# A graph network kernel: when three engines read its end-of-program flag, and which engine issues the last outputs

## The chip, the cores and the metric

The kernel runs on one core of a Trainium2 chip. The metric is the device time of one execution in microseconds. Three runs of the kernel before took 475.0, 475.29 and 475.76 us; their median is 475.29.

A core has five engines with an instruction queue each: TensorE (PE; its weight loads are shown as PEld), VectorE (DVE), ScalarE (ACT), GpSimd (POOL) and SyncE (SP, which only issues transfers and waits). They meet through semaphores. A "q" behind a name (SPq) marks an instruction of the engine's sequencer: a DMA issue, a wait, a branch, a register load.

## The reference

There are 2500 nodes of 256 features and 80000 edges. A layer norm and a relu are followed by three layers of an edge convolution that averages over incoming edges, and a product with the concatenation of all layers is added to the input:

```
def _edge_conv(x, src, dst, W, b):
    m = concatenate([x[dst], x[src] - x[dst]], axis=-1) @ W + b
    s = segment_sum(m, dst, num_segments=N)
    cnt = segment_sum(ones, dst, num_segments=N)
    return s / maximum(cnt, 1.0)[:, None]

h = maximum(_layernorm(x), 0.0)
xs = [h]
for W, b in ((W0, b0), (W1, b1), (W2, b2)):
    h = relu(_edge_conv(h, src, dst, W, b))
    xs.append(h)
return x + concatenate(xs, axis=-1) @ Wf + bf
```

## The kernel before

The 2500 nodes make 20 tiles of 128 rows (the last has 68), which go through the kernel as ten pairs. `by_windows` builds the matrix of edge counts from one-hot products of short stretches of the sorted edge list, keeps it in DRAM for the later layers, and runs the three layers as matrix products with it. That path holds only where no stretch has more edges than it was given room for. At about 182 us `shares` writes a single integer, the tile `missing`: 0 if all edges were found, 1 if not. At the end of the program (line 1441) `values_load` loads it into a register of each of the five engines, and `tc.If` (line 1442) branches on it: if it is 1, the engines run `general`, a slow path that holds for any graph; if it is 0, as here, they jump over that path to the closing waits. Line 1438 marks that jump as likely for TensorE, VectorE and ScalarE.

The order of work on each engine is written out by hand. `PEo`, `DVEo`, `POOLo`, `ACTo` and `SPo` are wrappers whose calls stay in program order on their engine; all of these calls are shown at line 282, the wrapper's. Calls through `nc` or the plain engines, the flag loads among them, are placed by the framework where their inputs allow: SyncE and GpSimd load the flag at 183 us already, in the midst of the program, and ScalarE, VectorE and TensorE behind their last computations. Transfers signal their landing on eight semaphores that are used in turn; before an issue the queue waits until the previous transfer on that semaphore has landed.

The change is in the last loop of `by_windows` (lines 1410 to 1431) and in `gnn_kernel`. The loop goes over the ten pairs in the order 8, 9, 0, 1, 2, 3, 7, 6, 5, 4 of `orders[L]`. For pair `q` TensorE multiplies its two tiles of the last layer's result with the last part of `Wf`, each tile into half a bank (the last pair into two banks); VectorE (`add_to_acc`) adds each product, scaled, into the tile's place in `acc`; and SyncE issues the transfer of that tile to `out`, 128 KB:

```
for k in range(2):
    t = 2 * q + k
    add_to_acc(t, po[k])
    n = P if t < NT - 1 else LAST
    SPo.dma_start(out[t * P:t * P + n, :], acc[:n, t, :])
```

During the first four pairs ScalarE and VectorE still prepare the operands of later ones. ScalarE has nothing to do after that.

Of the kernel before, what the change touches and what calls it, by code (L numbers as in the profile page):

```python
# [313 lines left out]
def by_windows(ctx: ExitStack, tc: tile.TileContext, x, src, dst, Ws, bs, Wf, bf, out, missing):  # L314
    nc = tc.nc
    PE, DVE, ACT, POOL, SP = nc.tensor, nc.vector, nc.scalar, nc.gpsimd, nc.sync
    PEo, DVEo, POOLo, ACTo, SPo = (InOrder(tc, e) for e in (PE, DVE, POOL, ACT, SP))
    P = 128
# [29 lines left out]
    Q = NT // 2  # L348
# [23 lines left out]
    def bank():  # L372
        return ps[-1].tile([P, 512], F32, name="bank")


    acc = const.tile([P, NT, D], F32, name="acc")
# [136 lines left out]
    behind = pp.tile([P, WG * P], F32, name="behind")  # L513
# [510 lines left out]
    def split_in_blocks(q, whole=True):  # L1024
        two = [block().rearrange("p c n -> p (c n)") for _ in range(2)]
        return Split(q, [two[0][:, :2 * D], two[0][:, 2 * D:], two[1][:, :2 * D]], whole)
# [93 lines left out]
    def times(to, split, i, forms):  # L1120
        for c in range(DC):
            for k in range(3):
                PEo.matmul(to, split.parts[k][:, c, i * P:(i + 1) * P], forms.parts[k][:, c, :],
                           start=(c == 0 and k == 0), stop=(c == DC - 1 and k == 2))

    def add_to_acc(t, po):
        DVEo.scalar_tensor_tensor(acc[:, t, :], po, share[:, t:t + 1], acc[:, t, :], op0=OP.mult, op1=OP.add)
# [211 lines left out]
    def split(q):  # L1339
        tile_ = stage.tile([P, 4 * GS], F32R, name="staged")  # L1340
        Split(q, [tile_[:, k * 2 * D:(k + 1) * 2 * D] for k in range(3)])

    begun = []
    for l in range(1, L):
# [7 lines left out]
        for i in range(Q + LAG):  # L1352
            if 0 < i <= Q:
                lone.make(i - 1)
            if i < Q:
                q = order[i]
                n = Nodes(l, q)
# [53 lines left out]
    for i, q in enumerate(order):  # L1411
        po = bank()
        po = [po[:, :D], bank()[:, :D] if i == Q - 1 else po[:, D:]]
        for k in range(2):
            if q in PLAIN:
                for c in range(DC):
                    PEo.matmul(po[k], hT[:, c, (2 * q + k) * P:(2 * q + k + 1) * P], wfs[L][:, c, :],
                               start=(c == 0), stop=(c == DC - 1))
            else:
                times(po[k], splits[q], k, coming[0])  # L1420
        for k in range(2):
            t = 2 * q + k
            add_to_acc(t, po[k])
            n = P if t < NT - 1 else LAST
            SPo.dma_start(out[t * P:t * P + n, :], acc[:n, t, :])
        if i == 0:
            begun[0].rest()
        elif i == 1:
            split_in_blocks(3)
        elif i < 4:  # L1430
            split((5, 4)[i - 2])


def gnn_kernel(tc: tile.TileContext, x, src, dst, Ws, bs, Wf, bf, out):
    nc = tc.nc
    with tc.tile_pool(name="flag", bufs=1) as flag:
        missing = flag.tile([1, 1], I32, name="missing")
        tc.mark_branch_hint_location("again", "LikelyTaken",
                                     engines=[getattr(mybir.EngineType, e) for e in ("PE", "DVE", "Activation")])
        by_windows(tc, x, src, dst, Ws, bs, Wf, bf, out, missing)  # L1440
        again = nc.values_load(missing, min_val=0, max_val=1)
        with tc.If(again > 0, label="again"):
            general(tc, x, src, dst, Ws, bs, Wf, bf, out)

# [27 lines left out]
```

## Time and profile before

| | |
|---|---|
| median of three runs | 475.29 us |
| the profiled execution's own time | 475.97 us |
| its span, from its first to its last instruction | 474.0 us |
| TensorE clock granted | 0.998 |
| PE busy | 462.7 us, 98% |
| DVE busy | 380.5 us, 80% |
| ACT busy | 310.6 us, 66% |
| output issues on SyncE | 20, at 454.5 to 470.2 us, 287 / 386 / 2093 ns (least, median, most) |
| from issue to landing of an output | 1.8 / 1.9 / 2.0 us |

Times inside the execution count from the span's first instruction. The 1.97 us between the profiled execution's time and its span lie outside the instructions shown. "Busy" leaves out what a sequencer does alone. A DMA issue's duration is the time its queue is held, not the transfer's; the transfer runs behind it on 16 shared DMA engines, and its landing is told by its semaphore. The view of DMA queues lists packets by queue, those that bring the engines' own instructions among them, and their share of the time of all 16 DMA engines in the stretch looked at.

### The profile page before, as it was taken

The page shows a single profiled execution, that of the slowest core. Times are in us where ns is not written, and L with a number is a line of the kernel's source. Part 1 is how long each engine was busy: PE and PEld are TensorE (multiplying, and loading weights), DVE is VectorE, ACT ScalarE, POOL GpSimd, SP SyncE. Part 2 cuts the span into 40 slices and gives each one's busy share as a digit, 9 for nine tenths or more (in the row PEclk, how much of TensorE's full clock was granted, in tenths as well). Part 3 has the DMA queues.
Part 4 walks back from the last instruction along what each step waited for, and adds up shares of the span by engine and source line. Part 5 has one row for each costly group of instructions (what it writes and reads, how often), then busy time and mean ns, then how long its engine had stood idle before and what let it go on. Part 6 is the DMA issues. An engine that isn't in the chain of part 4 may idle for free.

```text
span 474.0 us, 7362 instructions
## 1 busy us (share of the span) xinstructions
PE 462.7 (98%) x2739; PEld 365.3 (77%) x2739; DVE 380.5 (80%) x699; ACT 310.6 (66%) x543; POOL 42.6 (9%) x66
## 2 busy tenths in 40 slices
PE   7999999999999999999999999999999999999994
PEld 3787888788778878877887877877788787688694
DVE  7988988799898873499987847876999687569794
ACT  4877677686664541378769857775777797497430
POOL 2674014300101001000000000000000000000000
PEclk9999999999999999999999999999999999999999
DMA  8320073991733707532178552010213955220024
GB/s 277 90 56 1 1 157 66 187 215 35 158 63 69 152 0 152 124 100 75 46 235 310 176 174 62 28 44 5 83 44 97 360 177 176 87 88 0 1 73 147
DMA packets 21775, 52.07 MB, mean 110 GB/s; under 512 B 1943, under 2 KB 12134, under 8 KB 21734
## 3 DMA queue, kind: packets, MB, share of 16 engines
q1 hardware_dynamic: 14950, 33.93, 21.9%
q0 software_dynamic: 5856, 16.51, 18.2%
q10 hardware_dynamic: 928, 1.11, 0.7%
q8 instruction: 22, 0.36, 0.3%
q14 instruction: 19, 0.16, 0.1%
HBM read 36.08 MB, written 15.46 MB: 109 GB/s over the span
## 4 chain that ended last, share of the span: by engine, by line
PE 88%; DVE 5%; POOL 3%; DMA 2%; issue 1%; ACTq 0%; DVEq 0%; POOLq 0%
PE bank L282 84%; PE pz L282 3%; DMA acc<-in_x_dram 2%; DVE acc L282 2%; POOL acc L282 1%; DVE st L282 1%; POOL es L282 1%; POOL ed L282 1%; DVE staged L282 1%; DVE tmp L282 0%; DVE zl L282 0%; DVE mv L282 0%; PE turned L282 0%; DVE kn L282 0%; DVE rs L282 0%
## 5 line engine op out<-in xcount | busy, mean ns | idle before, releaser
L282 ACT CAST block<-staged 128x1008 fp32r<-128x1008 bf16 x120 | 117.8, 1031 | 17.0 <-DVE staged L282 6.3
L282 PE MATMUL bank<-block,zh 128*128 128x504 f32 (+1 forms) x200 | 83.7, 419 | 0.0
L282 PE MATMUL bank<-a,zh 128*128 128x504 f32 (+1 forms) x200 | 81.7, 409 | 0.0
L282 ACT CAST a<-bank 128x480 fp32r<-128x480 f32 (+1 forms) x105 | 54.5, 561 | 39.0 <-PE bank L282 37.2
L282 PE MATMUL bank<-a,zl 128*128 128x504 f32 (+1 forms) x200 | 77.8, 389 | 0.0
L282 PE MATMUL bank<-block,zl 128*128 128x504 f32 (+1 forms) x200 | 77.3, 387 | 0.0
L282 DVE TENSOR_TENSOR one_m<-iota_m,key_m 128x2048 bf16<-128x2048 bf16 (+2 forms) x55 | 64.3, 1169 | 9.9 <-PE bank L282 9.7
L282 PE MATMUL bank<-block,sh 128*128 128x504 f32 x160 | 68.9, 431 | 0.0
L282 PE MATMUL bank<-block,staged 128*128 128x512 f32 (+1 forms) x288 | 63.5, 371 | 0.3 <-DVE staged L282 0.2
L282 PE MATMUL bank<-block,sl 128*128 128x504 f32 x160 | 62.6, 391 | 0.0
L282 PEld LDWEIGHTS bank<-block,staged 128*128 128x128 f32 x288 | 49.2, 188 | 11.4 <-DVE staged L282 1.6
L282 DVE TENSOR_TENSOR one_n<-iota_n,key_n 128x960 bf16<-128x960 bf16 (+2 forms) x110 | 51.4, 509 | 0.0
L282 DVE TENSOR_TENSOR block<-staged 128x1008 fp32r<-128x1008 bf16 x40 | 46.9, 1205 | 5.5 <-PE bank L282 4.2
L282 PEld LDWEIGHTS <-one_m 128*128 128x128 bf16 x834 | 37.4, 97 | 13.6 <-issue 7.6
L282 PEld LDWEIGHTS bank<-block,zh 128*128 128x128 f32 x200 | 37.6, 188 | 10.8 <-issue 2.5
L282 PEld LDWEIGHTS bank<-block,zl 128*128 128x128 f32 x200 | 37.6, 188 | 10.6 <-issue 3.5
L282 PE MATMUL bank<-one_n,one_m 128*128 128x120 bf16 x834 | 44.7, 204 | 0.1
L282 PEld LDWEIGHTS bank<-a,zh 128*128 128x128 f32 x200 | 37.8, 189 | 6.3 <-issue 0.2
L282 PEld LDWEIGHTS bank<-a,zl 128*128 128x128 f32 x200 | 37.8, 189 | 6.3 <-issue 0.2
L282 DVE TENSOR_TENSOR staged<-staged 128x1008 bf16<-128x1008 bf16 x40 | 27.1, 679 | 17.3 <-ACT block L282 16.9
L282 PE MATMUL pz<-wbf,hT 128*128 128x256 f32 x160 | 38.7, 387 | 0.5 <-DMA wbf<-in_L_gnn_Wf_dram 0.2
L282 PEld LDWEIGHTS bank<-block,sh 128*128 128x128 f32 x160 | 30.1, 188 | 10.4 <-issue 3.5
(163 smaller groups left out, 616.4 us busy)
## 6 DMA issues: line engine op xcount, KB each, us to landing
staged<-a_dram SPq DMA_DIRECT2D x52, 504.0 KB, 4.5
a_dram<-a POOLq DMA_DIRECT2D x20, 630.0 KB, 10.8
out_dram<-acc SPq DMA_DIRECT2D x19, 128.0 KB, 1.9
acc<-in_x_dram POOLq DMA_DIRECT2D x3, 640.0 KB
wbf<-in_L_gnn_Wf_dram SPq DMA_DIRECT2D x4, 256.0 KB, 12.6
acc<-in_x_dram SPq DMA_DIRECT2D x1, 896.0 KB, 9.8
acc<-in_x_dram ACTq DMA_DIRECT2D x1, 768.0 KB
wbf<-in_L_gnn_W_dram SPq DMA_DIRECT2D x3, 256.0 KB, 7.4
```

Source lines behind the costliest of these rows:

```text
L282: return self.tc.keep_in_program_order(call(*args, **kwargs))
```

## The change

The second output of each of the last four pairs is issued by ScalarE instead of SyncE. `by_windows` returns the last such issue of the pair next to last (the ninth in order, its second tile). The flag is loaded by a call that also returns the load instructions, and those on TensorE, VectorE and ScalarE get a dependence on that transfer: they wait until it has landed. The loads on SyncE and GpSimd, and the branch, are as before.

```diff
             t = 2 * q + k
             add_to_acc(t, po[k])
             n = P if t < NT - 1 else LAST
-            SPo.dma_start(out[t * P:t * P + n, :], acc[:n, t, :])
+            d = (ACTo if i >= Q - 4 and k else SPo).dma_start(out[t * P:t * P + n, :], acc[:n, t, :])
+            if i == Q - 2:
+                near_end = d
...
+    return near_end
...
-        by_windows(tc, x, src, dst, Ws, bs, Wf, bf, out, missing)
-        again = nc.values_load(missing, min_val=0, max_val=1)
+        near_end = by_windows(tc, x, src, dst, Ws, bs, Wf, bf, out, missing)
+        loads, (again,) = nc.values_load_multi_w_load_instructions(missing, min_val=0, max_val=1)
+
+        for d in loads:
+            if d.ins.engine in [getattr(mybir.EngineType, e) for e in ("PE", "DVE", "Activation")]:
+                tc.add_manual_dep(d.ins, near_end.ins.name,
+                                  mybir.DependencyInfo(mybir.DependencyClass.Sync, mybir.DependencyReason.DATA),
+                                  reason="behind the outputs")
         with tc.If(again > 0, label="again"):
             general(tc, x, src, dst, Ws, bs, Wf, bf, out)
```

## The prediction

> **What bounds the kernel now.** I read the page first, then the chain of waits at the end, then single rows of the last 10 us. Columns are the page's: start and length in us, engine, line, operation.
>
> ```profile
> span 474.0 us, 7362 instructions
> PE 462.7 (98%) x2739; PEld 365.3 (77%) x2739; DVE 380.5 (80%) x699; ACT 310.6 (66%) x543; POOL 42.6 (9%) x66
> ```
>
> TensorE is busy 98% of the span, so only its edges are open. The chain of waits from 460 us:
>
> ```profile
> 459.80 7.65 PE bank L282 x57
> 467.45 0.03 issue
> 467.47 0.48 DVE acc L282
> ```
>
> Computation ends at 467.95; the span ends at 474.0. These 6.05 us are outside every engine's busy time, and the change touches only them. SyncE's output issues, in order of time:
>
> ```profile
> 466.35 0.41 SPq L282 DMA_DIRECT2D out_dram<-acc  x1
> 466.85 2.09 SPq L282 DMA_DIRECT2D out_dram<-acc  x1
> 469.04 0.38 SPq L282 DMA_DIRECT2D out_dram<-acc  x1
> 469.51 0.61 SPq L282 DMA_DIRECT2D out_dram<-acc  x1
> 470.22 0.38 SPq L282 DMA_DIRECT2D out_dram<-acc  x1
> ```
>
> The issues follow each other at 0.50 us (466.35 to 466.85), while VectorE finishes a tile every 0.39 us in a burst; one takes 2.09 us instead of 0.40. The last, at 470.22, starts 2.26 us after its tile was ready. It lands 1.8 us later, at 472.0 (the trace's median from issue to landing is 1.9, its least 1.8); 2.0 us of closing waits and barriers end the span. Now the flag loads (L1441), the branch (L1442) and what follows it:
>
> ```profile
> L1441 ACTq TENSOR_LOAD <-missing x1: 563/563/563, 455.5 to 455.5; - x1
> L1441 PEldq TENSOR_LOAD <-missing x1: 520/520/520, 465.2 to 465.2; - x1
> L1441 DVEq TENSOR_LOAD <-missing x1: 546/546/546, 467.5 to 467.5; - x1
> ...
> L1442 PEldq COMPARE_BRANCH  x1: 398/398/398, 465.8 to 465.8; - x1
> L1442 PEldq EVENT_SEMAPHORE  x1: 51/51/51, 467.5 to 467.5; - x1
> L1442 DVEq COMPARE_BRANCH  x1: 84/84/84, 468.1 to 468.1; - x1
> L1442 DVEq EVENT_SEMAPHORE  x1: 21/21/21, 468.7 to 468.7; - x1
> L1442 SPq COMPARE_BRANCH  x1: 53/53/53, 470.6 to 470.6; - x1
> ```
>
> And the DMA queues in the 0.1 us from 466.9, with packets, MB and share of 16 engines' time:
>
> ```profile
> q1 hardware_dynamic: 36, 0.04, 107.4%
> q8 instruction: 1, 0.02, 101.0%
> ```
>
> One packet of instructions starts there, 16 KB; 101.0% of 16 x 0.1 us is 1.62 us on one DMA engine. TensorE branches at 465.80 and this packet starts at 466.96, 1.16 us later. ScalarE's branch (456.09) is followed by an 8 KB packet after 1.09 us, VectorE's (468.11) after 1.19, SyncE's (470.65) after 1.05. So I read it as the fetch that TensorE's taken branch starts. An output is spread over all 16 DMA engines; of the output issued at 465.86, by the trace's records of completions, 15 of 16 came by 467.65 and the last at 469.75. One engine was stuck for 2.1 us, and SyncE's issue with it.
>
> **The change part by part.** Nothing before 462 us is touched: TensorE and VectorE get no work, so the tile sums end where they did: pair nine (i = 8) at 466.54 and 466.94, pair ten at 467.33 and 467.96.
>
> *Flag loads behind the landing.* The named output is the second of pair nine. The three loads wait until it has landed, so the branches and their fetches go behind that. Removed: the 2.09 us issue becomes 0.40, 1.69 us gained on SyncE's queue; VectorE's fetch at 469.30 goes too, and with it the 0.61 of the issue beside it, 0.22 gained.
>
> *Second outputs on ScalarE.* ScalarE's last computation ends at 457.01, so its queue is empty. It issues four DMAs; its two issues at the start of the span took 0.40 and 0.49 us for larger transfers, SyncE's 0.33 to 0.41 for these: 0.40 taken, 0.33 to 0.49 kept. SyncE keeps four of these eight, which it can start when each tile is ready. Both queues start an issue 0.03 us behind the sum (462.99 after 462.96). Pair nine's second goes at 466.97, pair ten's second at 467.99 instead of 470.22: 2.23 us earlier. That contains the 1.69 and 0.22 above; the split itself brings the remaining 0.32. A transfer on the other queue lands 1.8 us after its issue, as on SyncE (1.7 to 2.0): 469.79.
>
> *What comes in its place.* SyncE is done early: its last issue is 467.36 to 467.76, its branch 467.80, its own 8 KB fetch 1.05 us later, 468.85. The last output's packets run about 0.9 to 1.4 us after their issue, 468.9 to 469.4. So the collision comes back in small. The nearest row is VectorE's fetch at 469.30: 8 KB, 39.5% of 16 x 0.1 us, which is 0.63 us on one DMA engine, and it lengthened the issue by 0.22. Bounds 0 and 0.63; I take 0.30, nearer to the row. Last landing 470.09.
>
> *The wait's own chain.* Queued behind each load is only the branch and the closing semaphores; for these waits SyncE, which ends the program. The named output lands at 466.97 + 1.8 = 468.77; load 0.56 (rows 0.52 to 0.56), gap 0.11, branch at 469.44. From branch to next instruction VectorE took 0.61, TensorE at most 1.68 (465.80 to 467.48, where it also waited for its last matmul, ended 467.45). So TensorE reports between 470.05 and 471.12; I take 470.3. SyncE asks for TensorE's semaphore 0.96 us after it saw the last landing (472.02 to 472.98): 471.05. Hidden at zero by these waits; without that cover each microsecond costs one. The three fetches start at 470.5, behind the last landing.
>
> *A rule against it.* The Trainium skill's "Runtime: NRT & Kernel Launch", section "Instruction fetch mechanics", says a taken branch whose target isn't in the window of loaded instructions waits for a DMA fetch before it goes on. VectorE's row differs: its next instruction ran at 468.71, before its fetch began at 469.30. By the rule TensorE would report only behind a fetch of 1.62 us, about 472.2, and the end would be some 1.1 us later than by the row.
>
> *Sum.* Last issue -2.23, collision +0.30: **-1.93 us**, last landing 470.09, closing 2.0, span 472.1. The profiled execution took 475.97 with its span of 474.0; the median of the runs shown is 475.29. 475.29 - 1.93 = **473.4**.
>
> **The rivals.**
>
> 1. *The closing chain becomes the bound.* For it: load, branch and fetch now stand in series, and loads of this flag on SyncE and GpSimd took 1.58 and 1.20 us at 182 us. Against: those fell into a time of busy DMA queues, and three rows near the end are at 0.52 to 0.56. Price: 468.77 + 1.58 + 0.11 + 1.68 = 472.14, plus the 1.02 from 472.98 to 474.0: span 473.16, time **474.4**.
> 2. *The change doesn't move the fetch.* It could be TensorE's regular one: 257 TensorE rows lie between this packet and the one before (447.86), about the distance of earlier ones. Against: all rows were dispatched before the branch, and the four branches have the same 1.05 to 1.19 us. Then the named output itself, issued at 466.97, is stuck; the stuck one landed 4.2 us after its issue (466.85 to 471.02), so 471.1; load, gap and branch 1.28, rest 1.02: span 473.4, time **474.7**.
> 3. *Slower: the load stands ahead of pair ten's matmuls on TensorE.* Only the outputs and sums are held to the written order; the load isn't. Against: now 0.11 us lie between its end and the branch on TensorE, 0.08 on VectorE, so nothing was dispatched between. Price: TensorE resumes at 469.33; 24 matmuls of 0.125 us (24 in 2.99) end at 472.3, sum 0.48, landing 1.8, closing 2.0: 476.6 span, **477.9**. It decides from about three matmuls behind the load: the end is as before when the last sum ends at 470.2.
>
> **How the numbers follow.** Forecast 0.75 (its own range 472.8 to 474.0: landing 1.7 to 2.0, collision 0 to 0.63, ScalarE's issue), rival 1 0.08, rival 2 0.11, rival 3 0.06. The time is the forecast's, 473.4. The range 472.6 to 474.7 takes in rival 1 and half of rival 2. A change within 0.2% (0.95 us, down to 474.34) can't be told from none. Faster: 0.75, half of rival 1 and 0.03 of rival 2, 0.82. Same: 0.12. Slower: 0.06.
>
> **What would show it.** Right: no output issue over 0.7 us after 462; ScalarE's last issue near 467.99; the 16 KB packet behind 470; TensorE's flag load at 468.8; the last closing wait for a landing near 470.1; the 8 KB packet of SyncE's branch near 468.85. Wrong: a 16 KB packet still at 467; an end set by SyncE waiting for TensorE; a flag load followed by matmuls; landings on ScalarE's queue over 2.2 us.

## The result, and the profile after

The changed kernel took 473.67 us (median of 12 runs, 473.32 to 474.37), the kernel before 475.11 us (12 runs, 474.78 to 475.76). The ratio is 0.9971, 95% interval 0.9963 to 0.9979: 1.44 us less, where 1.93 was forecast, and inside the stated range. Run again beside another set of 16 runs of the kernel before (475.17), it took 473.26 us (5 runs), ratio 0.9961 (0.9947 to 0.9974).

The chain of waits at the end of the changed kernel:

```profile
459.97 6.72 PE bank L282 x50
466.69 0.03 issue
466.72 0.48 DVE acc L282
```

The last sum ends at 467.20 here, at 467.96 in the profile before. Nothing in the change touches what lies ahead of it, and over the profiles of this case that end lies anywhere from 467.13 to 468.27. So 0.75 of the 2.3 us between the two spans (474.0 and 471.7) lies ahead of the last sum, well within that scatter of 1.14. The number to compare is the **tail**, from the end of VectorE's last sum to the end of the span: 6.04 us before, 4.54 after, 1.50 less. Each kernel's tail is that of one profiled execution; the difference agrees with the 1.44 of the medians. All times below with a plus sign count from the end of the last sum.

The last output issues, from the timeline of the changed kernel:

```profile
465.82 0.33 SPq L282 DMA_DIRECT2D out_dram<-acc  x1
...
466.21 0.34 ACTq L282 DMA_DIRECT2D out_dram<-acc  x1
...
466.60 0.33 SPq L282 DMA_DIRECT2D out_dram<-acc  x1
...
467.23 0.34 ACTq L282 DMA_DIRECT2D out_dram<-acc  x1
```

No issue is held; the last starts at +0.03 instead of +2.26. The flag loads and the branch, grouped by line:

```profile
L1444 ACTq TENSOR_LOAD <-missing x1: 618/618/618, 468.0 to 468.0; - x1
L1444 DVEq TENSOR_LOAD <-missing x1: 612/612/612, 468.1 to 468.1; - x1
L1444 PEldq TENSOR_LOAD <-missing x1: 572/572/572, 468.1 to 468.1; - x1
...
L1451 SPq COMPARE_BRANCH  x1: 53/53/53, 467.0 to 467.0; - x1
...
L1451 PEldq COMPARE_BRANCH  x1: 398/398/398, 468.8 to 468.8; - x1
...
L1451 PEldq EVENT_SEMAPHORE  x1: 51/51/51, 469.2 to 469.2; - x1
```

All three loads stand at 468.05 to 468.11, just behind the landing of the named output (+0.77, 467.97). TensorE reports at 469.24. The fetches behind the three branches have no output beside them any more. Two of them stand in the DMA queues from 469.9 for 0.1 us; the third started at 469.86, also behind the last completion:

```profile
q8 instruction: 1, 0.02, 77.2%
q14 instruction: 1, 0.01, 32.0%
```

But SyncE, done early, branches at 466.98, and its own fetch, 1.54 us later, stands among the last output's packets (queues from 468.5 for 0.1 us; q10 is ScalarE's queue):

```profile
q14 instruction: 1, 0.01, 19.6%
q10 hardware_dynamic: 9, 0.00, 12.0%
```

That packet of 8 KB takes 19.6% of 16 x 0.1 us, 0.31 us. Of the last output's 16 completions, 15 came by +1.86 and one at +2.55. SyncE's closing waits follow that one.

### The profile page after: what moved, and what is told of

The parts are those of the page before. It is cut to its first block, busy times and chain, and to the rows that moved or that the text cites. A ratio compares the mean times of both kernels' runs of the same rounds, so it can differ in the third digit from the quotient of the medians.

```text
span 471.7 us, 7365 instructions
## 1 busy us (share of the span) xinstructions
PE 463.1 (98%) x2739; PEld 365.6 (77%) x2739; DVE 380.3 (81%) x699; ACT 310.5 (66%) x543; POOL 43.2 (9%) x66
## 3 DMA queue, kind: packets, MB, share of 16 engines
q10 hardware_dynamic: 1504, 1.63, 1.1%
## 4 chain that ended last, share of the span: by engine, by line
PE 88%; DVE 5%; POOL 3%; DMA 2%; issue 1%; ACTq 0%; DVEq 0%; POOLq 0%
PE bank L282 84%; PE pz L282 3%; DMA acc<-in_x_dram 2%; DVE acc L282 2%; POOL acc L282 1%; DVE st L282 1%; POOL ed L282 1%; POOL es L282 1%; DVE staged L282 1%; DVE tmp L282 0%; DVE zl L282 0%; DVE mv L282 0%; PE turned L282 0%; DVE kn L282 0%; DVE rs L282 0%
```

## The experiments

The trace's records of completions carry the reading of nearly every run, so here they are for the last output, with the tail of each profiled execution and the median of its runs. An output has 16 completions; those that came well behind the others stand under "late". Runs 1 to 4 stand beside a median of 475.23 us of the kernel before (23 runs), runs 5 to 8 beside 475.17 (16 runs).

```
                                   last output        late        tail   median   ratio to before
                                   issued  completed  completion                 (95% interval)
before                             +2.26   +3.84-4.05 none        6.04   475.11
changed                            +0.03   +1.63-1.86 +2.55       4.54   473.67   0.9971 (0.9963-0.9979)
1 wait only                        +0.37   +1.98-2.22 none        4.21   473.60   0.9961 (0.9948-0.9974)
2 split only                       +0.03   +1.67-1.84 +2.32,3.07  5.07   474.19   0.9977 (0.9968-0.9986)
3 first outputs on ScalarE         +0.03   +1.54-1.77 none        3.77   473.58   0.9959 (0.9946-0.9971)
4 wait on TensorE only             +0.36   +1.95-2.15 +3.17       5.16   474.82   0.9988 (0.9979-0.9997)
5 SyncE's load waits too           +0.03   +1.56-1.76 none        4.39   473.55   0.9965 (0.9953-0.9978)
6 wait on all but TensorE          +1.99   +3.59-3.81 none        5.80   474.87   0.9992 (0.9982-1.0003)
7 changed, again                   +0.03   +1.66-1.85 +2.25       4.24   473.26   0.9961 (0.9947-0.9974)
8 first outputs on ScalarE, again  +0.03   +1.55-1.77 none        3.77   472.71   0.9954 (0.9939-0.9968)
```

**1. The wait alone.** All outputs stay on SyncE.

```diff
-            d = (ACTo if i >= Q - 4 and k else SPo).dma_start(out[t * P:t * P + n, :], acc[:n, t, :])
+            d = SPo.dma_start(out[t * P:t * P + n, :], acc[:n, t, :])
```

> All 20 outputs on SyncE, the three flag loads behind the landing of the second output of pair nine. The yardstick is the tail, from the end of VectorE's last sum to the end of the span: 6.04 us in the kernel before, 4.54 in the changed one. Theory (the stall of 2.09 us is TensorE's fetch, and what the changed kernel pays at the end is SyncE's own fetch running into ScalarE's last output): no issue over 0.7 us; the last issue starts 0.37 us behind the last sum, lands 1.8 us later; SyncE's fetch comes 1.05 us behind its branch, when the last packets are out. Tail 4.15 us, 0.4 shorter than the changed kernel, some 473.2 us of time. Rival (the stall comes from many issues back to back on one queue): a stall of about 2 us stays, tail 6.0, time as before.

Tail 4.21 against 4.15 expected, median 473.60 against 473.2. The output issues of the whole run, grouped:

```profile
L282 SPq DMA_DIRECT2D out_dram<-acc x20: 287/390/405, 454.3 to 468.1; - x20
```

Ten issues back to back, the longest 0.405 us: the queue's pace makes no stall, and the rival falls. The wait alone brings 1.63 us in the medians, between the 1.44 and the 1.91 that the whole change brought in two sets, and its tail is no longer than the changed kernel's.

**2. The split alone.** The flag loads are as in the kernel before: the loop that adds their dependence is left out.

```diff
-        for d in loads:
-            if d.ins.engine in [getattr(mybir.EngineType, e) for e in ("PE", "DVE", "Activation")]:
-                tc.add_manual_dep(d.ins, near_end.ins.name,
-                                  mybir.DependencyInfo(mybir.DependencyClass.Sync, mybir.DependencyReason.DATA),
-                                  reason="behind the outputs")
```

> ScalarE issues every second output of the last four pairs, the flag loads stand as in the kernel before. Theory (TensorE's fetch): the 16 KB packet stays about 1.2 us behind TensorE's branch, near the time when the sums of pair ten run; one DMA engine works off its backlog at 0.32 us an output; last landing 3.2 to 3.8 us behind the last sum, tail 5.1 to 5.9 us, 0.1 to 0.9 shorter than before (time 474.2 to 475.0). Rival (back-to-back issues): with two queues no stall, tail 4.2 to 4.5, time as the changed kernel or better.

A tail of 5.07, just under the range of the theory and above that of the rival. The landings tell them apart:

```profile
SPq L1446 <- SPq L1446: 3.3, 4, 2.3
```

In the view of what SyncE waited for, its closing waits (L1446 here) stand for 3.3 us, 2.3 of them in one piece. The last four outputs had one completion each at +2.12, +2.45, +2.76 and +3.07, 0.31 to 0.33 us apart, the others by +0.34, +0.75, +1.13 and +2.32. That is what one DMA engine would show that works off a backlog; the records of completions don't name the engine. No issue was held this time, so the rival's "no stall" is true of the queue and the theory's backlog of the landing. TensorE's fetch came later here, 2.12 us behind its branch, and took 0.95 us instead of 1.62 (queues from 468.2 for 0.1 us):

```profile
q8 instruction: 1, 0.02, 59.2%
```

SyncE's last issue had ended at 467.99, before that packet started at 468.25, so the later fetch is enough to explain that SyncE was not held. ScalarE's last issue started 0.05 us behind the packet and took its usual 0.34. Whether the split would spare an issue under which the packet starts stays open. The split alone is worth 1.04 us, the wait alone 1.63, and both 1.44 and 1.91 in two sets: they don't add up, since either alone already leaves no issue held.

**3 and 8. The other half on ScalarE.** ScalarE issues the first output of each of the last four pairs, so that SyncE issues the very last one and branches behind it.

```diff
-            d = (ACTo if i >= Q - 4 and k else SPo).dma_start(out[t * P:t * P + n, :], acc[:n, t, :])
+            d = (ACTo if i >= Q - 4 and not k else SPo).dma_start(out[t * P:t * P + n, :], acc[:n, t, :])
```

> As the changed kernel, but ScalarE issues the first output of each of the last four pairs and SyncE the second, so that SyncE's branch comes behind the very last issue. Theory (SyncE's fetch met the last output and cost 0.69 us): the last issue starts 0.03 us behind the last sum and lands 1.8 us later with all 16 completions within 0.3 us; SyncE's fetch starts 1.05 us or more behind its branch, when the last packets are out. Tail 3.8 us, 0.7 shorter than the changed kernel, time about 473.0. Rival (a last landing 2.5 us behind its issue is ScalarE's queue or chance, not the fetch): if ScalarE's queue, its earlier outputs land late as well; if chance or the fetch is not avoided, tail 4.2 to 4.6, time as the changed kernel.

> The version with the first output of each of the last four pairs on ScalarE and the second on SyncE, again, beside the changed kernel. Theory: tail 3.8, 0.5 to 0.8 us less time than the changed kernel in the same call. Rival (the gain over the changed kernel was chance of one profile): less than 0.2 us between the two medians.

Both profiles have a tail of 3.77, as expected, and no late completion; the first set's median is 473.58, where about 473.0 was expected. The DMA queues of the second of them, from 467.1 to 468.9, hold one packet of instructions, SyncE's, at +1.46:

```profile
q1 hardware_dynamic: 257, 0.23, 38.4%
q10 hardware_dynamic: 145, 0.13, 21.6%
q14 instruction: 1, 0.01, 1.6%
```

It starts as the last output is completing, and delays nothing. In the one set where both stand beside the changed kernel the medians are 472.71 and 473.26: 0.55 us less. This is the fastest version of the study, 0.9954 of the kernel before; its interval overlaps that of the changed kernel, so the order of the two rests on that 0.55 and on the tails, 3.77 twice against 4.54 and 4.24. Against the wait alone (run 1, tail 4.21) the medians of the one set show nothing, 473.58 and 473.60; the six runs of version 3 spread from 472.63 to 474.02.

**4. The wait on TensorE only**, all outputs on SyncE as in 1.

```diff
-            if d.ins.engine in [getattr(mybir.EngineType, e) for e in ("PE", "DVE", "Activation")]:
+            if d.ins.engine == mybir.EngineType.PE:
```

> All outputs on SyncE; only TensorE's flag load waits for the second output of pair nine, VectorE's and ScalarE's stand as before. Theory: TensorE's 16 KB fetch alone made the 2.09 us; VectorE's branch stays right behind the last sum, its 8 KB fetch comes 1.2 us behind that branch and meets the last outputs on one DMA engine for 0.3 to 0.7 us: tail 4.4 to 4.9, time 473.4 to 473.9. Rival (VectorE's load or branch holds SyncE: a view of waits names VectorE's branch line as what ended SyncE's wait): the 2 us stall stays, tail 6.0.

```profile
L282 SPq DMA_DIRECT2D out_dram<-acc x20: 287/388/406, 454.4 to 468.2; - x20
```

The stall is gone with VectorE's load and branch where they were, so the rival falls: they don't hold SyncE. The tail, 5.16, misses its range of 4.4 to 4.9, and the median, 474.82, its 473.4 to 473.9. The queues between 469.4 and 469.7 show why:

```profile
q1 hardware_dynamic: 39, 0.02, 25.5%
q14 instruction: 2, 0.02, 21.9%
```

Two packets of instructions, behind VectorE's and SyncE's branches, 0.25 us apart (+1.64 and +1.89), and a completion that comes 1.02 us behind the other 15. One fetch had been reckoned with. Against 1 (4.21) VectorE's and ScalarE's waits are worth 0.95 us of tail, and 1.2 of the medians. TensorE's wait by itself removes the whole stall and brings only 0.41 us in the medians, for what the two 8 KB fetches then delay takes much of it back.

**6. The wait on all but TensorE**, all outputs on SyncE.

```diff
-            if d.ins.engine in [getattr(mybir.EngineType, e) for e in ("PE", "DVE", "Activation")]:
+            if d.ins.engine in [getattr(mybir.EngineType, e) for e in ("DVE", "Activation")]:
```

> All outputs on SyncE; VectorE's and ScalarE's flag loads wait for pair nine's second output, TensorE's doesn't. Theory (TensorE's 16 KB fetch makes the stall): an issue of 1 to 2.1 us some 1.1 us before the last sum ends, one completion of several outputs over 1 us late; tail 5.3 to 5.9, time 474.6 to 475.1. Rival (VectorE's branch, or the three fetches together, make it): no issue over 0.7 us, tail 4.2 to 4.5, time 473.6.

The issue that is held, and the queues from 466.9 for 0.1 us:

```profile
466.77 2.02 SPq L282 DMA_DIRECT2D out_dram<-acc  x1
```

```profile
q1 hardware_dynamic: 31, 0.03, 96.0%
q8 instruction: 1, 0.02, 91.1%
```

The stall is back, 2.02 us against 2.09, with the 16 KB packet 1.24 us behind TensorE's branch, and two outputs with a single completion about 2 us late. Tail 5.80. Runs 4 and 6 settle whose load it is: the stall goes when TensorE's flag load alone is moved, and stays when that one alone is left where it was. That the packet holds the issue, and not the load or the branch ahead of it, is read from the times: the issue ended 0.37 us behind the end of the packet here (468.80 after 468.43) and in the kernel before (468.95 after 468.57), although the packets took 1.46 and 1.62 us. The two waits without TensorE's bring 0.30 us in the medians, with an interval that takes in no gain at all: TensorE's wait brings little without the others, and the others little without TensorE's. The view of waits of the kernel before puts 1.9 us of SyncE's waiting down to VectorE's branch line; VectorE's branch came well behind the stall here.

**5. SyncE's load waits too**, with the outputs as in the changed kernel.

```diff
-            if d.ins.engine in [getattr(mybir.EngineType, e) for e in ("PE", "DVE", "Activation")]:
+            if d.ins.engine in [getattr(mybir.EngineType, e) for e in ("PE", "DVE", "Activation", "SP")]:
```

> As the changed kernel, ScalarE still issuing the last output, but SyncE's flag load waits for the landing of pair nine's second output as well, so that SyncE's branch comes some 1.9 us later. Theory (the one late completion of the last output is SyncE's own fetch): all 16 completions of the last output come within 0.3 us, the last 1.9 us behind the last sum instead of 2.55; but SyncE now comes to its first closing wait only 2.2 us behind the last sum and has 22 of them: tail 4.3 to 4.5 us, time as the changed kernel. Rival (ScalarE's queue lands its last output late): one completion 0.5 us or more behind the others as before, at 2.5 us.

All 16 completions of the last output come by +1.76, on ScalarE's queue as in the changed kernel: the late one was SyncE's fetch. The tail is 4.39 all the same, since SyncE now loads, checks and branches first, reaches its first closing wait at +2.16 and has 22 of them before it. This is as expected, and no gain.

**7. The changed kernel again.**

> The changed kernel again, unedited, so that it stands on one chip beside the version that issues the first outputs on ScalarE. Theory: one completion of the last output 0.5 to 0.8 us late, tail 4.5, time 0.3% under before. Rival (that late completion is chance): tail 3.8 to 3.9 here.

One completion of the last output came at +2.25, 0.40 behind the others; the tail is 4.24. The lateness isn't chance, but it is smaller than the 0.5 expected, and that tail lies between what the theory and the rival gave.

## Why the prediction was right, and where it was off

- **The stall is TensorE's fetch, and goes with its flag load.** Right: runs 4 and 6 show that it goes with TensorE's load, and the common 0.37 us from the packet's end to the issue's end ties it to the fetch. Rival 2 is out: the 16 KB packet moved with the branch, 1.17 us behind it in the changed kernel.
- **Last issue 2.23 us earlier.** Right: +2.26 became +0.03.
- **Collision with SyncE's own fetch, 0.30 taken between 0 and 0.63.** The mechanism was right (runs 3, 5 and 8 take the late completion away by moving SyncE's branch) and the size was off: 0.69 in the first profile, just over the upper bound, and 0.40 in the second. This is the mis-sized term of the sum. SyncE's fetch also started later than the 1.05 us behind its branch that were reckoned with: 1.54 us in the first profile, 1.20 in the second. The upper bound was the length of a fetch packet; a completion can come later than by the packet's own time (0.31 us there). It carries most of the miss: without the 0.39 between 0.69 and 0.30 the tail would have been 4.15, where the sum gave 4.11.
- **The split brings 0.32.** As a step by itself this stands only if SyncE's branch comes behind the last issue: the start of that issue goes from +0.37 to +0.03 between runs 1 and 3, and the tail from 4.21 to 3.77. As the change places it, it brings nothing against run 1 (4.54 and 4.24 against 4.21), for the collision takes it back. The sum had both terms, 0.32 and 0.30.
- **VectorE's fetch, 0.22.** Too small as a price of that part: run 4 shows 0.95 where VectorE's fetch comes close to SyncE's. In the sum this didn't matter, since both are gone.
- **The closing chain is hidden.** Right, rival 1 is out: TensorE reported at +2.04 (+2.34 forecast) and SyncE asked at +3.53. The rule of the Trainium skill's "Runtime: NRT & Kernel Launch" ("Instruction fetch mechanics"), that a taken branch waits for a fetch if its target isn't in the window of loaded instructions, put TensorE's report behind its fetch. That wait didn't come for TensorE either: its next instruction ran 0.46 us behind the start of its branch, 0.7 us before the 16 KB packet started. GpSimd's row was overlooked, and it goes the other way: it branched at 183.78 in the kernel before, an 8 KB packet of instructions started at 188.37, and its next instruction ran at 189.93, 1.56 us behind that start, a distance that is 1.56 to 1.57 in all ten profiles. That is what a wait for the fetch would look like; that the packet is GpSimd's is read from this distance alone. No run shows on which engines the target stood in the window, so the rule itself is neither refuted nor shown; the 1.1 us that the prediction reckoned by it for TensorE did not come.
- **Rival 3** didn't come: the loads stand directly before the branches.
- **The forecast of 1.93 against 1.44 and 1.91 in the medians.** The tail gained 1.50 and 1.80 in the two profiles of the changed kernel, against the one profile of the kernel before. The difference between the two follows the collision, 0.69 and 0.40. That 1.91 comes so near to 1.93 is in part luck: its profile still has a collision 0.10 above the term.

ScalarE's wait was not tried by itself, nor the kernel without a branch.

## What to carry to other kernels

Look at the time between the last computation and the end of the span by itself: where one transfer issue takes many times its usual length, look for a packet of instructions on the DMA queues and for a taken branch 1.0 to 1.7 us before it (2.1 once here). In this program the branches of TensorE and VectorE had to come so late that their fetches met no output: waiting for the landing of the output two before the last was enough. SyncE's wait for it brought nothing, as SyncE also makes the closing waits (run 5); there it helped that SyncE issued the last output itself, so that its fetch came too late to delay it. A split over two queues that frees one engine early can bring that engine's branch forward into the transfers it was meant to speed up.

## What the runs showed of the hardware that was not expected

One packet of 8 KB of instructions made an output's completion 0.40 and 0.69 us late while it took 0.45 and 0.31 us itself, and two of them (0.58 and 0.47) made one 1.02 us late. TensorE's packets of 16 KB took 0.95 to 1.62 us near the end of the program. Where such a packet started 0.1 to 0.2 us behind the start of SyncE's issue (the kernel before and run 6), that issue took 2.0 to 2.1 us and ended 0.37 us behind the packet's end. In run 2 no issue of SyncE was under way when the packet started, and none was held. A single late completion of the 16 is enough to delay an output: among the last ten outputs of each profile the other 15 came within 0.25 us of each other, but for the last output of run 2, which had two late ones. On TensorE, VectorE, ScalarE and SyncE an instruction behind the branch that had no other wait ran 0.45 to 0.61 us after the branch began, before the fetch started (1.0 to 1.7 us after it, 2.1 once); GpSimd's ran only behind a packet.
